# Sign weights held behind the mask addition of the same step: one change to VectorE's order in a fused attention and feed-forward kernel

## The chip, the cores and the metric

The kernel runs on one core of a Trainium2 chip. A core has five engines with an instruction queue each: TensorE (PE, matrix products, with PEld for its weight loads), VectorE (DVE), ScalarE (ACT), GpSimd (POOL) and SyncE (SP, which here only issues DMA transfers). Work between engines is ordered by semaphores. The metric is the device time of one launch in microseconds; lower is better.

## The reference

An image batch of 8 x 32 x 32 x 384 goes through two layers. `x` is float32 throughout.

```python
# layer 0: windowless attention with relative positions, 6 heads of 64
x = x + _L0_conv_ref(_gn(x), qkv_w, qkv_b, proj_w, proj_b, rel_pos_h, rel_pos_w)
# layer 1: causal single-head attention of width 384, then the feed-forward
t = _to_tokens(x)                        # 8 x 1024 x 384
t = t + _L1_attn_ref(_ln_t(t), Wq, Wk, Wv)
t = t + _L1_ffn_ref(_ln_t(t), W1, b1, W2, b2)

def _binarize_weights_groupwise(W):      # 5 groups along the output features
    for g in range(NUM_GROUPS):
        wg = W[g * gs:(g + 1) * gs]
        z = wg - wg.mean()
        Wb = Wb.at[g * gs:(g + 1) * gs].set(sign(z))   # rows beyond 5 * gs stay zero

def _bitlinear(x, W, b):
    y = einsum('btc,oc->bto', x, _binarize_weights_groupwise(W)) + b
    return _quantize_activations_groupwise(y)          # 8 bits, 5 groups along the batch
# feed-forward: _bitlinear to 1536 features, exact GELU, _bitlinear back to 384
```

With 8 images and 5 groups along the batch, each of images 0 to 4 is a group of its own, and images 5 to 7 belong to none: their quantised result stays zero. So the feed-forward matters for images 0 to 4 alone.

## The kernel before

**Order of the images.** One loop goes over the images in the order 5, 0, 1, 2, 3, 4, 6, 7 (`ORDER`); images 0 to 4 (`B_FFN = 5`) also run the feed-forward. Image 5 comes first since it has no feed-forward, so that there is time to make the sign weights.

**Layer 0** (`layer0`, `attend0_fast`). Queries and keys are projected (L438), relative positions are written to DRAM and gathered back as tiles `r` (L484 to L524), values are projected (L536). Attention goes over three pairs of heads and two halves of the tokens. One such half-stage has 8 tiles of scores (L588 for the product, L592 for the positions), their exponentials on ScalarE (L598), additions of the 8 exponentials on VectorE (L603, L605), and the product with the values (L613). The sums over the tiles and their reciprocals of the half-stage before are done between the additions (L622 to L640): L631 multiplies into a PSUM bank `den`, L635, L427 and L428 read it. A residual image is loaded (L106) and `pb` added to it on POOL (L567). Then comes the projection (L386).

**Layer 1** (`attention1`, `attend1_fast`). Layer norm, queries (L734), values (L386 too, as `f_v`), and then eight steps `c` of 128 keys. A step computes its scores (L775), adds the causal mask to the diagonal tile on VectorE (L780), takes exponentials (L782), and lets `values(c - 2)` multiply probabilities with values (L788) and update the residual on VectorE (L789 to L791). Between them stands one step of the next image's group norm (`other`; L338 to L349).

**The sign weights** (`binarize`) are a generator that runs once, in small steps. It loads the raw weights in three pieces of 1.5 MB on POOL's queue (L232), sums them by group on VectorE (L250, 20 sums), forms the means (L256, L258 on POOL, L262), loads the same pieces again, and writes signs over them with two VectorE instructions a block (L272, L273, 30 pairs; L279 clears a rest). Each finished piece is stored to the DRAM tensors `w1s` and `w2s` by SP (L280). It is created in layer 0 of image 5, at pair 2 (`signs.append(binarize(pools))`), and then each step of layer 1 of images 5 and 0 takes two of its steps:

```python
for work in 2 * signs:
    next(work, None)
```

The feed-forward of each image loads the sign weights from DRAM (`sign_weights`, POOL, L862 to L865) and multiplies with them at L895 and L936.

**What sets the order.** The program is written in one order, and a scheduler then places the instructions on each engine's queue by what it reckons to be ready; an instruction can come to stand far earlier than the place where it is written, if its operands allow it. `with tc.issue_after(ins):` adds an edge: each instruction traced inside on the engine of `ins` is placed behind `ins` in that engine's queue, with no semaphore. On a queue, instructions go in order.

**Buffers.** Tiles of 12 KB a partition (`pools.flat`, `pools.image`) come from one pool of 11: `x`, `q`, `k`, `v`, the four `r`, `oT`, `far`, the layer-1 tiles, the raw and sign pieces, the feed-forward's weights and hidden tiles. A tile waits for the last use of the tile that had its buffer before. All PSUM tiles come from one pool of 8 banks (`o_tile`).

Of the kernel before, what the change touches and what calls it, by code (L numbers as in the profile page):

```python
# [15 lines left out]
ALU = mybir.AluOpType  # L16
# [3 lines left out]
P = 128  # L20
# [55 lines left out]
def conv_attn_hybrid(  # L76
# [19 lines left out]
    nc = tc.nc  # L96
# [48 lines left out]
    maskT = const.tile([P, P], F32, name="maskT")  # L145
# [159 lines left out]
    def stages(pools):  # L305
# [120 lines left out]
        def check(total, reciprocal, i):  # L426
            nc.vector.tensor_reduce(seen[:, 0, i : i + 1], total, AX.X, ALU.add)  # L427
            nc.vector.tensor_reduce(seen[:, 1, i : i + 1], reciprocal, AX.X, ALU.add)  # L428
# [333 lines left out]
        def attend1_fast(xt, b, q, xT, v, other, start):  # L762

            room = [pools.flat(f"pr1_{b}_{i}") for i in range(2)]
            tot = pools.small.tile([P, NJ], F32, tag="tot1", name=f"tot1_{b}")
            rt = pools.small.tile([P, NJ], F32, tag="rt1", name=f"rt1_{b}")

            def scores(c):
                at = sum(NJ - i for i in range(0 if c < 3 else 3, c)) * P
                pr = room[c >= 3][:, at : at + (NJ - c) * P]  # L770
                for half in range(c // 4, 2):
                    sc = pools.o_tile(f"s1_{b}_{c}_{half}")
                    lo = max(0, c * P - half * 512)
                    for k in range(NC):
                        nc.tensor.matmul(  # L775
                            sc[:, lo:], xT[:, c // 4, k, ts(c % 4, P)], q[:, half, k, lo:],
                            start=(k == 0), stop=(k == NC - 1),
                        )
                    if half == c // 4:
                        nc.vector.tensor_tensor(sc[:, ts(c % 4, P)], sc[:, ts(c % 4, P)], maskT, ALU.add)  # L780
                    at = half * 512 + lo - c * P
                    nc.scalar.activation(pr[:, at : at + 512 - lo], sc[:, lo:], AF.Exp)  # L782
                return pr

            def values(j):
                av = pools.o_tile(f"av1_{b}_{j}")
                for c in range(j + 1):
                    nc.tensor.matmul(av[:, : C + 1], prs[c][:, ts(j - c, P)], v[:, c, :], start=(c == 0), stop=(c == j))  # L788
                nc.vector.tensor_copy(tot[:, j : j + 1], av[:, C : C + 1])  # L789
                nc.vector.reciprocal(rt[:, j : j + 1], tot[:, j : j + 1])  # L790
                nc.vector.scalar_tensor_tensor(  # L791
                    xt[:, j, :], av[:, :C], rt[:, j : j + 1], xt[:, j, :], ALU.mult, ALU.add
                )

            prs = []
            for c in range(NJ):
                prs.append(scores(c))
                next(other, None)
                for work in 2 * signs:
                    next(work, None)  # L800
                if c >= 2:
                    values(c - 2)
            if b < B_FFN:
                for work in signs:
                    assert next(work, None) is None
                signs.clear()
            start()
            values(NJ - 2)
            values(NJ - 1)
            check(tot, rt, b * PER_IMAGE + PER_IMAGE - 1)  # L810
# [143 lines left out]
        signs = []  # L954
# [92 lines left out]
```

## Time and profile before

| what | before |
|---|---|
| median of 3 runs | 2371.3 us (2369.2 to 2372.32) |
| the profiled execution | 2370.05 us |
| its span | 2367.9 us |
| mean granted PE clock | 0.996 |
| layer 0 of image 5, pairs 1 and 2, from 110 to 193 us | PE's windows are in the prediction |
| sums of raw weights (L250) | 20, from 114.7 to 255.2 us |
| signs (L272, L273) | 30 pairs, from 264.2 to 507.8 us |
| layer 1 steps of image 5 | from 242 to 289 us |
| layer 1 steps of image 0 | from 488 to 536 us |
| first use of the sign weights (L895) | 542.18 us |

The profile's page has, in this order: busy time of each engine with its share of the span, the span in 40 slices (digits are tenths), the DMA queues, the chain of waits that ended last, the costliest groups of instructions, and the DMA issues with the median time from issue to landing. A group reads: line, engine, operation, output<-input, sizes, count, busy us, mean ns of one, idle us of the engine just before it and what ended most of it. Lines are those of the kernel file before; in the changed file, lines from L780 on stand 2 or 3 further down. PE's matmul ends are modelled, and adjacent records overlap.

### The profile page before, as it was taken

What the parts mean: (1) busy time and instruction counts of PE and PEld (TensorE: products, weight loads), DVE (VectorE), ACT (ScalarE), POOL (GpSimd) and SP (SyncE); (2) the same over time, 40 slices, a digit from 0 to 9 for tenths busy, and PEclk for the clock granted to TensorE, in tenths of its full rate; (3) what the DMA queues carried; (4) which work ended last, traced back from release to release, by engine and by line L of the source; (5) the groups of instructions that cost most, each with busy time, mean ns of one, the idle gap of its engine ahead of it and who ended that gap; (6) DMA issues with size and microseconds to landing.
All of it is one profiled execution on the core that took longest, in us unless ns stands there. A gap on an engine that the chain in (4) does not pass through costs nothing.

```text
span 2367.9 us, 26177 instructions
## 1 busy us (share of the span) xinstructions
PE 2332.1 (98%) x9442; PEld 1291.8 (55%) x9442; DVE 1431.8 (60%) x2302; ACT 1042.0 (44%) x1763; POOL 312.2 (13%) x421
## 2 busy tenths in 40 slices
PE   7989999999999999999999999999999999999998
PEld 3445544557644577445684455764457744554454
DVE  3486548754678346685455873567844668525851
ACT  3442146226564146561374622656424656115520
POOL 0320004000230001220002300023000122001300
PEclk9989999999999999999999999999999999999999
DMA  7421363220441011621107311054101172017100
GB/s 163 146 63 54 134 118 96 81 80 1 114 113 68 14 41 44 162 63 40 41 1 145 96 67 41 1 116 114 65 14 41 44 162 63 1 47 137 57 1 29
DMA packets 154795, 169.99 MB, mean 72 GB/s; under 512 B 113408, under 2 KB 126048, under 8 KB 153120
## 3 DMA queue, kind: packets, MB, share of 16 engines
q1 hardware_dynamic: 134416, 98.93, 17.5%
q0 software_dynamic: 17184, 69.22, 9.7%
q8 instruction: 77, 1.26, 0.2%
q10 hardware_dynamic: 3056, 0.08, 0.1%
q14 instruction: 62, 0.51, 0.1%
HBM read 75.38 MB, written 42.47 MB: 50 GB/s over the span
## 4 chain that ended last, share of the span: by engine, by line
PE 95%; DVE 2%; DMA 1%; POOL 0%; issue 0%; ACT 0%; SPq 0%; DVEq 0%; POOLq 0%; ACTq 0%
PE f_s L588 13%; PE f_av L613 13%; PE f_qk L438 11%; PE f_s L775 8%; PE f_av L788 8%; PE f_y L936 7%; PE f_y L895 7%; PE f_pj L386 5%; PE f_v L386 5%; PE f_v L536 5%; PE f_q L734 5%; PE f_s L592 3%; PE f_rel L484 2%; PE f_pt L314 1%; DVE f_sum L605 1%; PE f_den L631 0%
## 5 line engine op out<-in xcount | busy, mean ns | idle before, releaser
L598 ACT ACTIVATE f_pr<-f_s 128x512 f32<-128x512 f32 x768 | 413.8, 595 | 72.3 <-PE f_s L592 64.1
L588 PE MATMUL f_s<-f_q,f_k 64*128 64x512 f32 x1536 | 404.7, 600 | 11.9 <-DVE seen L427 11.9
L605 DVE TENSOR_TENSOR f_sum<-f_sum,f_pr 128x1024 f32<-128x1024 f32 x288 | 364.4, 1265 | 22.4 <-DVE rt L635 0.6
L613 PE MATMUL f_av<-f_pr,f_v 128*64 128x512 f32 x1536 | 339.4, 594 | 0.0
L592 PE MATMUL f_s<-f_r,unit 64*128 64x512 f32 x768 | 311.5, 797 | 0.0
L438 PE MATMUL f_qk<-f_gnT,wqkv_sb 128*128 128x512 f32 x576 | 258.8, 602 | 1.5 <-DVE f_gnT L349 1.5
L588 PEld LDWEIGHTS f_s<-f_q,f_k 64*128 64x128 f32 x1536 | 148.1, 188 | 140.7 <-issue 74.1
L613 PEld LDWEIGHTS f_av<-f_pr,f_v 128*64 128x64 f32 x1536 | 106.3, 137 | 196.4 <-issue 192.4
L775 PE MATMUL f_s<-f_q,f_lnT 128*128 128x512 f32 (+3 forms) x576 | 195.9, 488 | 0.0
L788 PE MATMUL f_av<-f_v,f_pr 128*128 128x385 f32 x576 | 195.3, 486 | 0.0
L438 PEld LDWEIGHTS f_qk<-f_gnT,wqkv_sb 128*128 128x128 f32 x576 | 108.4, 192 | 144.2 <-issue 131.7
L524 POOL DMA_DIRECT2D f_r<-f_far x192 | 102.5, 536 | 462.3 <-DVE f_far L519 418.9
L782 ACT ACTIVATE f_pr<-f_s 128x512 f32<-128x512 f32 (+3 forms) x96 | 47.1, 491 | 263.8 <-DVE f_s L780 217.6
L788 PEld LDWEIGHTS f_av<-f_v,f_pr 128*128 128x128 f32 x576 | 108.2, 190 | 77.3 <-issue 11.5
L775 PEld LDWEIGHTS f_s<-f_q,f_lnT 128*128 128x128 f32 x576 | 102.0, 190 | 77.8 <-issue 54.1
L899 ACT ACTIVATE f_h<-f_y,b_sb 128x256 f32<-128x256 f32 x240 | 100.9, 471 | 67.3 <-PE f_y L895 67.3
L906 DVE TENSOR_REDUCE am<-f_h 128x1 f32<-128x1024 f32 (+2 forms) x80 | 71.6, 947 | 96.1 <-ACT f_h L899 96.1
L734 PE MATMUL f_q<-f_lnT,wqk 128*128 128x512 f32 x288 | 127.5, 592 | 0.0
L386 PE MATMUL f_pj<-wproj_sb,f_oT 128*128 128x384 f32 x384 | 127.3, 488 | 0.0
L592 PEld LDWEIGHTS f_s<-f_r,unit 64*128 64x128 f32 x768 | 76.9, 188 | 91.2 <-issue 90.7
L386 PE MATMUL f_v<-wv_sb,f_lnT 128*128 128x384 f32 x384 | 126.5, 486 | 0.0
L536 PE MATMUL f_v<-wqkv_sb,f_gnT 128*128 128x384 f32 x384 | 125.1, 486 | 0.0
(153 smaller groups left out, 3018.6 us busy)
## 6 DMA issues: line engine op xcount, KB each, us to landing
f_far<-f_far SPq DMA_DIRECT2D x48, 512.0 KB, 3.3
f_r<-f_far POOLq DMA_DIRECT2D x192, 128.0 KB, 3.9
f_r<-f_far SPq DMA_DIRECT2D x192, 128.0 KB, 3.2
f_gnT<-in_xT SPq DMA_DIRECT2D x24, 512.0 KB, 4.6
f_x<-in_x SPq DMA_DIRECT2D x32, 384.0 KB, 8.1
out_y<-f_x POOLq DMA_DIRECT2D x28, 384.0 KB, 4.5
f_far<-f_far SPq DMA_DIRECT2D x128, 64.0 KB, 5.1
f_w1a<-w1s POOLq DMA_DIRECT2D x5, 1536.0 KB, 6.9
```

What stands on the lines that cost most here:

```text
L386: nc.tensor.matmul(ps[:, :C], xT[:, k, ts(j, P)], w[:, k, cols], start=(k == 0), stop=(k == NC - 1))
L438: nc.tensor.matmul(made[half], wqkv_sb[:, i, ts(m, P)], xT[:, i, ts(half, 512)], start=(i == 0), stop=(i == NC - 1))
L536: nc.tensor.matmul(ps, keys[:, i, j // 2, j % 2], wqkv_sb[:, i, 2 * C :], start=(i == 0), stop=(i == NC - 1))
L588: nc.tensor.matmul(sc[par], k[rows[par], p, ts(c, P)], q[rows[par], p, ts(half, 512)], start=True, stop=False)
L592: last_matmul[0] = nc.tensor.matmul(sc[par], unit[rows[par], c // 2 % 2].rearrange("i h w -> i (h w)"), r[2 * (c // 4) + c % 2][rows[par], ...
L598: last_exp[0] = nc.scalar.activation(pr[:, ts(par, 512)], sc[par], AF.Exp).ins
L605: adds.append(nc.vector.tensor_tensor(total, total, pr, ALU.add).ins)
L613: last_matmul[0] = nc.tensor.matmul(av[ts(par, HD), :], v[:, c, ts(2 * p + par, HD)], pr[:, ts(par, 512)], start=(c == 0), stop=(c == NJ - 1),
L734: nc.tensor.matmul(ps, wqk[:, k, ts(m, P)], xT[:, half, k, :], start=(k == 0), stop=(k == NC - 1))
L775: nc.tensor.matmul(sc[:, lo:], xT[:, c // 4, k, ts(c % 4, P)], q[:, half, k, lo:], start=(k == 0), stop=(k == NC - 1),)
L788: nc.tensor.matmul(av[:, : C + 1], prs[c][:, ts(j - c, P)], v[:, c, :], start=(c == 0), stop=(c == j))
L895: nc.tensor.matmul(ps, w1k[i // 2][:, ts(m, P)], xs[i % 2][:, half, i // 2, :], start=(i == 0), stop=(i == 2 * NC - 1))
```

## The change

The 2 steps of the sign weights that a step of layer 1 takes are traced inside `issue_after` of that step's mask addition. So each of their VectorE instructions is placed behind that addition on VectorE's queue. Their POOL and SP instructions (loads, all-reduce, stores) get no such edge. At the end of image 0's steps, the check that the generator is used up also lets it run out.

```diff
@@ scores(c)
                     if half == c // 4:
-                        nc.vector.tensor_tensor(sc[:, ts(c % 4, P)], sc[:, ts(c % 4, P)], maskT, ALU.add)
+                        masked[0] = nc.vector.tensor_tensor(
+                            sc[:, ts(c % 4, P)], sc[:, ts(c % 4, P)], maskT, ALU.add
+                        ).ins
@@ attend1_fast
-            prs = []
+            prs, masked = [], [None]
             for c in range(NJ):
                 prs.append(scores(c))
                 next(other, None)
-                for work in 2 * signs:
-                    next(work, None)
+                with tc.issue_after(masked[0]):
+                    for work in 2 * signs:
+                        next(work, None)
                 if c >= 2:
                     values(c - 2)
             if b < B_FFN:
                 for work in signs:
-                    assert next(work, None) is None
+                    assert all(done for done in work)
                 signs.clear()
```

## The prediction

> **What bounds the kernel now.** I read the page's busy shares and chain first, then the waits of the stretch in which PE has holes, then PE's and VectorE's timelines there, last a table of windows.
>
> ```profile
> PE 2332.1 (98%) x9442; PEld 1291.8 (55%) x9442; DVE 1431.8 (60%) x2302; ACT 1042.0 (44%) x1763; POOL 312.2 (13%) x421
> ...
> PE   7989999999999999999999999999999999999998
> ...
> PE 95%; DVE 2%; DMA 1%; POOL 0%; issue 0%; ACT 0%; SPq 0%; DVEq 0%; POOLq 0%; ACTq 0%
> ```
>
> PE is busy 98% of the span and carries 95% of the chain, so only what stops or slows PE counts. Apart from the start and the end, one slice of forty is below nine tenths: the third, 118 to 178 us. The waits from 95 to 160 us (waiting line, releaser: total us, times, longest):
>
> ```profile
> DVE sums_w L250 <- DMA f_w<-in_w1T: 18.9, 2, 13.9
> ...
> PE f_s L588 <- DVE seen L427: 11.9, 2, 7.4
> ```
>
> PE waits twice for VectorE, and VectorE waits twice for a load of raw feed-forward weights. PE's timeline (start, us, line, idle before it), then VectorE's:
>
> ```profile
> 113.40 1.02 PE L588 MATMUL f_s<-f_q,f_k 64*128 64x512 f32 x2
> 121.77 1.22 PE L588 MATMUL f_s<-f_q,f_k 64*128 64x512 f32 x1 [7.36 <-DVE seen L427]
> ...
> 144.72 2.08 PE L588 MATMUL f_s<-f_q,f_k 64*128 64x512 f32 x4 [4.54 <-DVE seen L427]
> ```
>
> ```profile
> 98.94 1.84 DVE L605 TENSOR_TENSOR f_sum<-f_sum,f_pr 128x1024 f32<-128x1024 f32 x1
> 114.71 0.79 DVE L250 TENSOR_REDUCE sums_w<-f_w 128x1 f32<-128x614 f32 x1 [13.92 <-DMA f_w<-in_w1T]
> ...
> 121.55 0.17 DVE L427 TENSOR_REDUCE seen<-f_den 128x1 f32<-128x16 f32 x1
> ...
> 132.62 4.09 DVE L250 TENSOR_REDUCE sums_w<-f_w 128x1 f32<-128x307 f32 x10 [5.00 <-DMA f_w<-in_w1T]
> ...
> 144.40 0.17 DVE L427 TENSOR_REDUCE seen<-f_den 128x1 f32<-128x16 f32 x1
> ```
>
> VectorE stands from 100.8 to 114.7 at a weight sum (L250) whose load POOL issued only at 107.34. Behind it are the additions of L605 and the reduction L427, which frees the PSUM bank that PE's next score tile needs. PE starts again 0.2 to 0.3 us after each L427. The windows compare these two half-stages of image 5 (scores of one pair and half, then values) with the same two of image 0:
>
> ```profile
> 110.02:136.65 26.63, 19.27 (x86) 10.07 (x85) 16.80 (x28) 12.29 (x19) 2.62 (x3) 0.87 0.36 130
> 136.65:160.06 23.41, 18.88 (x86) 8.17 (x84) 22.46 (x24) 9.23 (x17) 7.15 (x10) 0.85 0.26 69
> 373.80:389.87 16.07, 16.07 (x87) 6.91 (x85) 13.43 (x15) 12.31 (x19) 6.51 (x8) 1.00 0.12 29
> 389.87:405.93 16.06, 16.06 (x87) 6.93 (x85) 15.53 (x18) 9.22 (x17) 6.99 (x9) 1.00 0.38 103
> ```
>
> The same PE work takes 26.63 + 23.41 = 50.04 us in image 5 and 16.07 + 16.06 = 32.13 us in image 0. The granted clock (third number from the end) is 0.87 and 0.85 against 1.00.
>
> **What the Trainium skill says.** "PSUM — Partial Sum Buffer", Engine vs sequencer instructions: VectorE's queue is strict FIFO. The trace agrees: L605 had its operands and still stood 13.92 us behind L250. "TensorE: Matmul & The Clock Gate", What's actually happening: an idle window of about 3.4 us halves PE's clock until PE has been busy as long. The trace agrees in kind: both holes are longer, and afterwards the rel-pos matmuls (L592), two at a time, take 1.45 us where they take 0.80 in image 0. "Trainium Kernel Development and Optimization", Key Constraints: transfers of SP, ACT and POOL share 16 DMA engines. So the moved transfers could delay others; their share between 300 and 560 us leaves room.
>
> **The change part by part.** The order in which the changed kernel is built shows that no L250 is left in layer 0: all 20 sums stand in layer 1 of image 5, each behind a mask addition (L780). The hold binds VectorE only; POOL's loads are free, and move where buffers come free.
>
> *Removed: the two stops.* 50.04 − 32.13 = **17.91 us**: 11.90 of idle (7.36 + 4.54) and 6.0 of slow matmuls after it. Next in line on VectorE are additions that ran without stopping PE in image 0. The second load of raw weights now stands on POOL behind pair 2's rel-pos pieces. Those are due before PE's scores at 142 (160.06 − 17.91); by image 0's spacing they land at about 137, and the weights have until 253.
>
> *Added to image 5's layer 1* (times of before; all shift together): 15 sums, 3.8 us for five of 614 columns and 2.0 each for the fives of 307 and 304: 7.8 us. Six pairs of sign instructions (L272, L273; 0.85 us a pair: 12.7 us for 15 pairs) leave for image 0: −5.1. VectorE was busy 29.72 of the 47 us from 242 to 289, now 32.4. Step by step:
> - Four sums (2.9 us) follow mask 0 at 245.3 and end at 248.2; L345 starts 0.5 late, but its square root waits for a table load until 249.44. Mask 1's scores come at 249.69: nothing lost.
> - One sum, the three normalisations and four sums of 307: mask 2 at 254.6 for 253.65. Its probabilities are first needed at 263.7: hidden.
> - Masks 3 to 6 wait for PE as before, within 0.3 us. The last sum ends at 265.0, the mean (POOL, 0.48 us) at 266; it is first used at 272.
> - Twenty sign instructions now stand as one block between mask 6 (271.7) and mask 7: 0.3 + 10 pairs at 0.74 start to start = 7.7 us. Mask 7 comes at 279.7 for 275.63, its exponential ends at 280.5. PE needs it for the last term of the last value tile, at about 288.5: 8 us of cover. The block also delays the residual update of value tile 4; its bank is next needed at 299.
>
> *Added to image 0's layer 1:* the six pairs, 5.1 us, fill VectorE's waits around masks 0 and 1 (1.79 + 2.32 + 1.89 us idle): mask 2 at 499.9 for 499.85. Nothing.
>
> *Buffers and queues.* The second piece of sign weights keeps its buffer through image 0's layer 0.
> - Image 0's residual load (SP, L106) must now wait for pair 1's pieces on POOL: 358.03 + 3.68 + 3.9 landing = 365.6 for 361.31. POOL's additions (L567) end at 382.3, one multiply at 384.5; POOL's next piece comes at 389.78: 5 us of cover.
> - The first load of sign weights for image 0 (POOL, L862) takes that buffer. It was issued at 455.93; now it waits for the piece (done 499.9) and its stores (at most 5.0 to land): issued 505, landed 512 (6.9). Behind it the next load waits for the last store: sign block done about 511, stored 516, landed 521 (4.5). PE needs them at 542.18 and 543.19: 30 and 22 us of cover. SP is empty from 428 to 508, so the moved stores push nothing.
>
> *Unknown:* whether the changed order stops PE for an instant that these sums do not show. Below: 1 us more gained, the spread of the half-stages being 0.1. Above: 4.1 us, the slip of mask 7, were its cover gone. I take 0, since each sum above ends before PE needs it.
>
> *Sum.* The profiled execution took 2370.05 us (span 2367.9 and 2.15 around it), 1.25 below the median of 2371.3. 2370.05 − 17.91 = 2352.1 for such an execution, so **2353.4 us** beside the median.
>
> **The rivals.**
> 1. *Only the idle time comes back.* PE runs slow in these half-stages for another reason, say the 86 to 195 GB/s of transfers: −11.9, **2359.4 us**. Against it: image 0 runs at clock 1.00 beside 103 GB/s, and in image 5 from 160 on the clock is 1.00 again.
> 2. *The stop moves.* VectorE stops in layer 1, at L279 or L262, for the sign load or the mean, with mask 7 and three residual updates behind it. It decides once VectorE resumes after 280 instead of 272; each us more costs PE one. 26 us late gives no change, **2371 us**. Against it: the mean is 6 us early, the sign load, free once the projection has read its buffer (209.5), is there by about 217.
> 3. *Slower: sign weights late for image 0.* The load that now shares a buffer with the second piece lands after 542, and PE waits for it; by the two stops of before, each us of idle brings half a us of slow matmuls (6.0 for 11.9), so it decides from 12 us late on, landing at 555. If the signs ended only with layer 1 (537.65, the last L360) and stores (4.4 + 3.3 + 5.0) and loads (6.9 + 4.5) went one after another, the second load would land at 562: 19 idle and 9 slow, less 17.9: 10 slower, **2381 us**. Against it: 30 and 22 us of cover, with stores and signs an engine apart.
>
> That the change doesn't do what it says is excluded by the built order. What stays open is only whether VectorE's waits end as reckoned.
>
> **How the numbers follow.** Forecast (17.9, with the bounds −1 and +4.1): 0.86. Rival 1: 0.08. Rival 2 within 0.2%: 0.03. Rival 3: 0.03. 0.2% is 4.7 us, about what a measurement of this kernel can tell from no change. The forecast and rival 1 are faster: 0.94; same 0.03; slower 0.03. The range begins at the forecast less 1 and the 2 us by which the runs lie under their median: 2350.5. It ends at 2359.6, which takes in the bound of 4.1 and rival 1.
>
> **What would show it.** In the profile after: no wait of PE's L588 for L427; the two half-stages at 16.1 us each, clock 1.00; all L250 after the first L780 with no idle before them for a transfer; mask 7 about 4 us later against PE; L862 of image 0 about 50 us later against PE, and no idle before f_y. Wrong if PE shows new idle in the layers 1 of images 5 or 0, or at the first f_y.

## The result, and the profile after

The changed kernel takes **2351.88 us** (median of 4 runs, 2350.82 to 2352.87) where the kernel before takes 2371.55 beside it: a ratio of 0.9919, 95% interval 0.9901 to 0.9936. That is 19.7 us less. In the profiled executions it is 2350.82 for 2370.05. In this file L784 is the exponential of layer 1, L790 the value product, L793 the residual update, L865 the first load of sign weights, L898 the first product of the feed-forward.

Of the page, the lines that answer to those of before (busy shares, PE's forty slices, the chain by engine):

```profile
PE 2324.9 (99%) x9442; PEld 1288.2 (55%) x9442; DVE 1433.9 (61%) x2302; ACT 1041.7 (44%) x1763; POOL 316.6 (13%) x421
...
PE   7999999999999999999999999999999999999998
...
PE 99%; DVE 1%; DMA 0%; issue 0%; ACT 0%; DVEq 0%
```

The 8 in the third slice is a 9, and PE's share of the chain is 99% for 95%. All of PE's waits in the whole span (waiting line, releaser: total us, times, longest):

```profile
PE f_gmean L336 <- DVE gmv L333: 10.9, 1, 10.9
PE f_bad L201 <- DVE worst L199: 1.9, 1, 1.9
PE f_qk L438 <- DVE f_gnT L349: 1.5, 1, 1.5
PE f_gvar L344 <- DVE gd L341: 0.7, 1, 0.7
PE f_den L631 <- DVE few L624: 0.3, 1, 0.3
```

The row of L588 for L427 (11.9 us) is gone, and none has come in its place: but for 0.3 us at L631, in another image, what is left lies at the start and the end. One more wait is gone with it, of 0.35 us: before, PE also waited at L631 at 192.59 us, ahead of the projection of image 5. The windows of the two half-stages of image 5 (the stretch and its length, busy us of PE, PEld, DVE, ACT, POOL with counts, granted clock, DMA share, GB/s):

```profile
108.75:124.81 16.06, 16.06 (x87) 6.81 (x85) 15.60 (x19) 12.27 (x19) 4.85 (x5) 1.00 0.40 126
124.81:140.86 16.05, 16.05 (x87) 6.80 (x85) 15.54 (x17) 9.17 (x17) 8.16 (x12) 1.00 0.63 187
```

50.04 us have become 32.11: **17.93 us**, where 17.91 were forecast, at clock 1.00, with 187 GB/s beside it in the second. Another 1.27 us lie ahead of these windows, at the start of the kernel (108.75 for 110.02), in work that the change does not touch. From 193 us to the end PE's products stay 19.0 to 20.1 us earlier than before, and the spans differ by 19.1, so nothing later in the kernel gained or lost more than a us. The rest is taken up at the end.

In layer 1 the sign weights' block stands where it was reckoned. Masks 6 and 7 before:

```profile
271.66 0.29 DVE L780 TENSOR_TENSOR f_s<-f_s,maskT 128x128 f32<-128x128 f32 x1
...
275.63 0.30 DVE L780 TENSOR_TENSOR f_s<-f_s,maskT 128x128 f32<-128x128 f32 x1
```

And after, VectorE, then ScalarE, then PE, from their timelines:

```profile
252.10 0.30 DVE L780 TENSOR_TENSOR f_s<-f_s,maskT 128x128 f32<-128x128 f32 x1 [0.28 <-PE f_s L775]
252.31 0.24 DVE L262 TENSOR_SCALAR mean_w<-mean_w 128x5 f32<-128x5 f32 x2
...
260.05 0.28 DVE L780 TENSOR_TENSOR f_s<-f_s,maskT 128x128 f32<-128x128 f32 x1
```

```profile
260.37 0.28 ACT L784 ACTIVATE f_pr<-f_s 128x128 f32<-128x128 f32 x1 [7.55 <-DVE f_s L780]
```

```profile
257.75 11.83 PE L790 MATMUL f_av<-f_v,f_pr 128*128 128x385 f32 x36
269.42 10.46 PE L438 MATMUL f_qk<-f_gnT,wqkv_sb 128*128 128x512 f32 x24
```

Mask 7 comes 7.95 us after mask 6 instead of 3.97, so 4.0 later; its exponential ends at 260.65; PE goes through its value products without a hole, and the last of them, which needs it, starts at about 269.1.

### The profile page after: what moved, and what is told of

It reads as the page before. It is cut to its first block, busy times and chain, and to the rows that moved or that the text cites. A ratio compares the mean times of both kernels' runs of the same rounds, so it can differ in the third digit from the quotient of the medians.

```text
span 2348.8 us, 26174 instructions
## 1 busy us (share of the span) xinstructions
PE 2324.9 (99%) x9442; PEld 1288.2 (55%) x9442; DVE 1433.9 (61%) x2302; ACT 1041.7 (44%) x1763; POOL 316.6 (13%) x421
## 4 chain that ended last, share of the span: by engine, by line
PE 99%; DVE 1%; DMA 0%; issue 0%; ACT 0%; DVEq 0%
PE f_s L588 14%; PE f_av L613 14%; PE f_qk L438 11%; PE f_s L775 8%; PE f_av L790 8%; PE f_y L939 7%; PE f_y L898 7%; PE f_pj L386 5%; PE f_v L386 5%; PE f_v L536 5%; PE f_q L734 5%; PE f_s L592 4%; PE f_rel L484 2%; PE f_pt L314 1%; PE f_den L631 0%; DMA f_gnT<-in_xT 0%
## 5 line engine op out<-in xcount | busy, mean ns | idle before, releaser
L588 PE MATMUL f_s<-f_q,f_k 64*128 64x512 f32 x1536 | 399.0, 595 | 0.0
L438 PE MATMUL f_qk<-f_gnT,wqkv_sb 128*128 128x512 f32 x576 | 257.4, 600 | 1.5 <-DVE f_gnT L349 1.5
L588 PEld LDWEIGHTS f_s<-f_q,f_k 64*128 64x128 f32 x1536 | 145.7, 186 | 127.4 <-issue 67.3
L790 PE MATMUL f_av<-f_v,f_pr 128*128 128x385 f32 x576 | 195.3, 486 | 0.0
L438 PEld LDWEIGHTS f_qk<-f_gnT,wqkv_sb 128*128 128x128 f32 x576 | 108.0, 191 | 143.2 <-issue 131.5
L784 ACT ACTIVATE f_pr<-f_s 128x512 f32<-128x512 f32 (+3 forms) x96 | 47.1, 491 | 267.7 <-DVE f_s L780 220.7
L790 PEld LDWEIGHTS f_av<-f_v,f_pr 128*128 128x128 f32 x576 | 108.2, 190 | 77.3 <-issue 11.5
```

Source lines behind the costliest of these rows:

```text
L438: nc.tensor.matmul(made[half], wqkv_sb[:, i, ts(m, P)], xT[:, i, ts(half, 512)], start=(i == 0), stop=(i == NC - 1))
L588: nc.tensor.matmul(sc[par], k[rows[par], p, ts(c, P)], q[rows[par], p, ts(half, 512)], start=True, stop=False)
```

## The experiments

Theory: the whole gain is that VectorE no longer waits, in layer 0 of image 5, for loads of raw weights with L427 queued behind the wait. Rivals: the signs' place carries part of it; the work of the sums, not their wait, held L427 up; the two stops of PE are one; and, for the size, whether slow matmuls go with the number of stops or with their length.

| kernel | median us | ratio to before (95%) | PE's new or remaining stops over 1 us |
|---|---|---|---|
| the change | 2351.88 | 0.9919 (0.9901 to 0.9936) | none |
| sums_held | 2352.0 | 0.9920 (0.9907 to 0.9934) | none |
| signs_held | 2371.07 | 0.9999 (0.9991 to 1.0008) | 6.87 and 5.77 |
| pieces23_held | 2362.65 | 0.9965 (0.9951 to 0.9978) | 7.28 |
| piece1_held | 2352.88 | 0.9931 (0.9918 to 0.9945) | 2.59 |
| resident_sums | 2353.18 | 0.9926 (0.9912 to 0.9939) | 1.65 |
| block_plus1 | 2351.84 | 0.9920 (0.9907 to 0.9934) | none |
| block_plus4 | 2351.38 | 0.9917 (0.9903 to 0.9930) | none |
| pinned_plus4 | 2361.16 | 0.9959 (0.9945 to 0.9972) | 6.26 |
| load_late5 | 2373.98 | 1.0013 (1.0006 to 1.0019) | 17.1 in four |
| load_again4 | 2361.45 | 0.9965 (0.9951 to 0.9978) | 6.26 |
| load_again7 | 2384.08 | 1.0056 (1.0042 to 1.0069) | 29.17 |
| after_busy_start | 2354.0 | 0.9930 (0.9915 to 0.9944) | at the start |

The medians of the kernel before, taken beside these kernels, lie between 2370.78 and 2371.55.

### Which half of the change carries it: sums_held and signs_held

`hold[0]` is the mask addition of the step; in one kernel the sums alone are traced behind it, in the other the signs alone.

```diff
+                with tc.issue_after(hold[0]):                          # sums_held
+                    nc.vector.tensor_reduce(part[...], w[...], AX.XY, ALU.add)
...
+                    with tc.issue_after(hold[0]):                      # signs_held
+                        nc.vector.tensor_scalar(above, wg, m, None, ALU.is_gt)
+                        nc.vector.scalar_tensor_tensor(wg, wg, m, above, ...)
```

> The kernel before with only the 20 sums (L250) behind the masks; the signs keep their free place. Theory (the whole gain is VectorE's wait for raw weights leaving layer 0 of image 5): no wait of L588 for L427, half-stages of 16.1 us, 2352 us as the changed kernel. Rival (the place of the signs carries part of it, since without a hold they come as 10 pairs before mask 7 and 10 pairs behind it): 2355 to 2360.

> The kernel before with only the signs (L272, L273) behind the masks; the sums stay in layer 0. Theory: both stops of PE stay (7.4 and 4.5 us, half-stages 26.6 and 23.4), 2371 us as before, within 1. Rival (the signs' place carries part of the gain): 2365 or less.

Measured: 2352.0 and 2371.07. The sums alone give the whole gain and the signs alone give none. So half of the change, the hold on the signs, does nothing for the time here: with or without it they fill VectorE's idle time.

### Whether the stops are separate: pieces23_held and piece1_held

The hold of sums_held under a condition; `held(on)` is `tc.issue_after(hold[0])` where `on` is true and nothing otherwise.

```diff
+                with held(not (n_out == FF and times[0] == 0)):        # pieces23_held
+                    nc.vector.tensor_reduce(part[...], w[...], AX.XY, ALU.add)
...
+                with held(n_out == FF and times[0] == 0):              # piece1_held
+                    nc.vector.tensor_reduce(part[...], w[...], AX.XY, ALU.add)
```

> The kernel before with the sums of the second and third loads behind the masks; the first load's 5 sums stay in layer 0. Theory (the two stops are separate): the stop of 7.4 us stays with its slow stretch (half-stage 26.6), the second half-stage falls from 23.4 to 16.1 but for what is left of the slow stretch: 2371.5 - 7.3 = 2364, 2363 to 2367. Rival (the second stop is only an echo of the first, VectorE never having caught up): PE stops a second time, 2369 to 2371.

> The kernel before with only the 5 sums of the first load behind the masks. The second load's 10 sums now stand in the half-stage after the one they stood in, behind its fourth addition, at about 135 us, and their load, issued at about 135, lands at about 142.5: VectorE stands some 7 us. Theory (a stop of PE is VectorE's standing time less some 6.5 us of cover, as in 13.9 less 7.4): PE stops 0 to 2 us, the first half-stage is 16.1 us, 2352 to 2355 us. Rival (each load waited for in layer 0 costs PE a stop of its own, 4.5 us and a slow stretch): 2359 to 2361.

The windows of the same two half-stages where the first load's sums stay in layer 0:

```profile
110.17:136.75 26.58, 19.30 (x87) 10.10 (x85) 21.51 (x27) 12.32 (x19) 2.63 (x3) 0.87 0.35 127
136.75:152.80 16.05, 16.05 (x86) 6.80 (x84) 15.52 (x19) 9.17 (x17) 7.18 (x10) 1.00 0.38 102
```

One half-stage has its stop as before (26.58 us, clock 0.87), the next is whole: 2362.65 us. The second stop was not an echo of the first. 7.28 of the 10.52 us that the first half-stage has too much are idle, 3.24 are matmuls that run slow.

Where the second load's sums stay instead, VectorE does stand, but PE does not at that place. VectorE's timeline, then PE's:

```profile
139.48 0.47 DVE L256 TENSOR_REDUCE sums_w<-f_w 128x1 f32<-128x307 f32 x1 [5.23 <-DMA f_w<-in_w1T]
```

```profile
175.46 0.29 PE L637 MATMUL f_den<-few,fold 128*64 128x16 f32 x4 [2.59 <-DVE few L630]
```

(L256 is L250, L637 is L631 in that file.) A wait of 5.23 us behind the fourth addition of a half-stage is covered there. What VectorE lost comes out at the end of layer 0, where nothing stands between its last additions and PE: 2.59 us. The time is 2352.88, in the range of the theory, though the theory had put the stop, if any, a half-stage earlier. No slow stretch follows: against the changed kernel's profile, PE's products lose 2.6 us at this stop, its idle time and no more. By the median only 1.0 us is left at the end of the kernel. In the profile, the fastest of five runs that spread over 5.2 us, most of the 2.6 us is made up bit by bit up to 1902 us and at no one place, so the runs do not tell this from the spread of executions.

### Wait or work: resident_sums

```diff
-                    part[...], w[:, :, ts(g, n_out // NG)], AX.XY, ALU.add
+                    part[...], there[:, :, ts(g, n_out // NG)], AX.XY, ALU.add
```

`there` is a view of the projection weights for the first two loads; the edges that hold the places are left out here. The loads themselves still run.

> The kernel before, but the 15 sums of the first two loads read the projection weights, which have long been on the chip, in tiles of the same shapes (so the means are of other numbers); they keep their places in VectorE's queue in layer 0, by an edge behind the same additions. It keeps their work there, 8 us, and takes only their wait away. Theory (the wait, not the work): no stop of PE, half-stages of 16.1 us, 2351 to 2354 us. Rival (the 8 us of work between the additions holds L427 up as well): PE stops, 2357 us or more.

Measured: 2353.18 us, no wait of the score products for VectorE. The sums' work, still between the additions of layer 0, cost PE one wait of 1.65 us at L631, and the median 1.3. The other 18 us were the wait.

### How far mask 7 may slip: block_plus1, block_plus4, pinned_plus4

```diff
                     for work in 2 * signs:
                         next(work, None)
+                    if b == ORDER[0] and c == 6:
+                        for i in range(4):          # 1 in block_plus1
+                            nc.vector.tensor_reduce(idle[:, i : i + 1], wqkv_sb.rearrange("p k c -> p (k c)"), AX.X, ALU.add)
```

> The changed kernel with one more VectorE instruction between masks 6 and 7 of image 5 (a sum over 3456 columns of a resident tile into a scratch tile, some 4.3 us by the rate of L250). Theory (mask 7 has 8.4 us of cover left: its exponential ends at 260.65, PE's last value product starts at 269.1): mask 7 comes 4.3 us later, PE does not stop, 2352 us within 1. Rival (the cover is less than reckoned, since PE or the residual updates wait earlier): 2354 to 2357.

> The changed kernel with four such instructions between masks 6 and 7 of image 5, some 17 us. Theory: mask 7 comes at 277, PE stops for 17 less 8.4 = 8.7 us at the last value product and then runs slow for some 3 us, as after the stop of 7.3 us in the run that kept only the first load's sums in layer 0: 2363 to 2364 us. Rival (the slow stretch grows with the idle time, half a us for each): 2365. Rival (mask 7 is not what PE waits for): 2352.

One more instruction moves mask 7 from 260.05 to 264.35 (0.7 us of this is the later start of that execution, 3.6 the instruction) and costs nothing, as reckoned. Four move it to 275.58, and the time is still 2351.38: the theory missed by 12 us. PE's timeline says why:

```profile
256.85 13.13 PE L790 MATMUL f_av<-f_v,f_pr 128*128 128x385 f32 x40
269.81 7.03 PE L438 MATMUL f_qk<-f_gnT,wqkv_sb 128*128 128x512 f32 x16
276.68 0.81 PE L790 MATMUL f_av<-f_v,f_pr 128*128 128x385 f32 x2
277.32 3.60 PE L438 MATMUL f_qk<-f_gnT,wqkv_sb 128*128 128x512 f32 x8
```

The program was not the same on PE. The scheduler put 16 projections of the next image ahead of the last value product. Presumably it reckoned with a late mask; the trace shows the order alone. The experiment had changed two things. So it was run again with these projections held behind the last value product, which gives PE's order of the changed kernel:

```diff
+                    with tc.issue_after(last_value[0]) if pools.fast and b == AFTER[ORDER[0]] else contextlib.nullcontext():
                         nc.tensor.matmul(made[half], wqkv_sb[:, i, ts(m, P)], ...)
```

> The changed kernel with the four more VectorE instructions between masks 6 and 7 (block_plus4), and PE's order held as in the changed kernel: the next image's projections (L438) stay behind the last value product, as they do there. Mask 7 then comes 15.5 us later than in the changed kernel, as it did in block_plus4. Theory (8.4 us of cover by that order): PE stops for 15.5 - 8.4 = 7.1 us at the last value product, then a slow stretch of some 3.2 us: 2362 us. Rival (mask 7 is not what PE waits for): 2352. Rival (the residual updates held with it stop PE later too): over 2364.

```profile
275.69 1.65 PE L793 MATMUL f_av<-f_v,f_pr 128*128 128x385 f32 x2 [6.26 <-ACT f_pr L787]
277.14 12.63 PE L441 MATMUL f_qk<-f_gnT,wqkv_sb 128*128 128x512 f32 x24
```

(L793 is the value product in that file, L441 the projection.) Mask 7 comes 22.45 us after mask 6 here, 14.5 more than in the changed kernel (the four took 14.9 us together, a little less than reckoned), and PE stops for 6.26 us: 8.2 us were covered. The 24 projections behind the stop take 12.63 us instead of 10.46: 2361.16 us, 9.3 over the changed kernel. So the 8 us of cover in the prediction hold, for a fixed order on PE. A scheduler that knows of the delay had another 7 us of work to put there.

### The price of late sign weights: load_late5, load_again4, load_again7

```diff
+            for _ in range(5 if b == 0 else 0):                        # load_late5
+                nc.gpsimd.tensor_tensor(a1, flat, flat, ALU.add)
...
+            for _ in range(7 if b == 0 else 0):                        # load_again7; 4 in load_again4
+                nc.gpsimd.dma_start(out=a1, in_=w1s[:, : 2 * half])
             nc.gpsimd.dma_start(out=a1, in_=w1s[:, : 2 * half])
```

`flat` is a view of the projection weights.

> The changed kernel, with POOL's load of w1a for image 0 put behind five additions on POOL that write its tile (3072 columns each, some 9.4 us by the rate of L567): issued at about 537.5 instead of 484.7, landed at about 544.5, where PE needs it at 522.6. It prices the prediction's slower rival. Theory now: 22 us of idle and a slow stretch of fixed length, some 3 us: 2377 us. Rival (the price that the prediction used, half a us of slow matmuls for each us of idle): 2352 + 22 + 11 = 2385 us. Rival (the weights are not what PE needs first): 2352.

Measured: 2373.98 us, near the theory's 2377, and for another reason: the load was issued at 525.23 and PE came to it at 544.45 without a wait. VectorE's timeline beside POOL's additions (the second fence):

```profile
502.12 11.80 DVE L376 TENSOR_SCALAR f_xn<-f_x,lmv,lrs 128x384 f32<-128x384 f32 x2
513.85 0.15 DVE L791 COPY tot<-f_av 128x1 f32<-128x1 f32 x1
513.92 5.86 DVE L376 TENSOR_SCALAR f_xn<-f_x,lmv,lrs 128x384 f32<-128x384 f32 x1
```

```profile
502.54 5.32 POOL L867 TENSOR_TENSOR f_w1a<-wqkv_sb 128x3072 fp32r<-128x3072 f32 x1
```

Each L376 takes 5.4 to 6.0 us where it takes 0.46 in the changed kernel: as long as one POOL addition. The Trainium skill, "SBUF — State Buffer", SBUF: two separate sides, says that GpSimd and certain VectorE instructions (in a two-port mode, or with two SBUF inputs) share one pair of ports as an exclusive lock, held for a whole instruction. The lengths agree with it; that L376 is of that kind no run here shows. PE waited 17.1 us for these L376 and what is queued behind them, so the run says nothing of late weights. The wait is in four stops (2.28, 5.39, 4.88 and 4.57 us) with 0.6 to 0.9 us of products between them. The delay was made again with transfers alone, each load of the tile waiting for the one before.

> The changed kernel with the load of w1a for image 0 done five times over into its tile, each behind the landing of the one before (some 7.4 us each; no POOL computation beside VectorE). The last lands at about 528, where PE needs it at 522.6. Theory (a slow stretch of about 3 us per stop): 5.6 us of idle and 3 of slow matmuls, 2360.5 us. Rival (half a us of slow matmuls for each us of idle): 2360.3, the same here. Rival (enough cover left): 2352.

> The same with eight loads, the last landing at about 550: 27.8 us of idle. Theory (the slow stretch after a stop is some 3 us, whatever the stop's length): 2351.9 + 27.8 + 3 = 2382.7 us. Rival (the price that the prediction used, half a us of slow matmuls for each us of idle): 2351.9 + 27.8 + 13.9 = 2393.6 us.

Measured: 2361.45 and 2384.08 us. PE's timelines (L900 is L898), first with five loads, then with eight:

```profile
530.17 0.77 PE L900 MATMUL f_y<-f_lnT,f_w1a 128*128 128x512 f32 x1 [6.26 <-DMA f_w1a<-w1s]
```

```profile
551.62 0.77 PE L900 MATMUL f_y<-f_lnT,f_w1a 128*128 128x512 f32 x1 [29.17 <-DMA f_w1a<-w1s]
552.19 0.63 PE L900 MATMUL f_y<-f_lnlo,f_w1a 128*128 128x512 f32 x1
...
556.03 0.52 PE L900 MATMUL f_y<-f_lnT,f_wrest 128*128 128x512 f32 x1
556.38 0.39 PE L900 MATMUL f_y<-f_lnlo,f_wrest 128*128 128x512 f32 x1
```

Products start 0.43 us apart until about 556.1 and 0.23 apart from there. The slow stretch is 4.5 us after 29.17 us of idle, and 4.5 us (530.17 to 534.7) after 6.26. The cost of each stop, by medians over the changed kernel, and beside it how much later than in the changed kernel's profile PE's products are behind the stop, less how much later they were ahead of it:

| stop | idle us | cost by medians | beyond the idle | later by the traces | beyond the idle |
|---|---|---|---|---|---|
| load_again4 | 6.26 | 9.6 | 3.3 | 8.6 | 2.3 |
| pinned_plus4 | 6.26 | 9.3 | 3.0 | 9.4 | 3.1 |
| pieces23_held | 7.28 | 10.8 | 3.5 | 10.5 | 3.2 |
| load_again7 | 29.17 | 32.2 | 3.0 | 31.5 | 2.4 |

The medians carry the spread of whole executions (1.4 to 4.9 us within these kernels), so the traces decide. For load_again7: its transposes ahead of the stop start at 520.98 where the changed kernel's start at 521.40, and its 14th product behind it at 556.84 where the changed kernel has it at 525.72; 31.12 and 0.42 make 31.54. A stop that stands alone costs its length and **2.3 to 3.2 us**, and at one and the same place as much for 29.17 us of idle as for 6.26. For the two load_again runs 2.1 of the 2.3 to 2.4 are the slow rate itself (11 products at 0.43 instead of 0.23). Why the two others cost 0.8 us more was not taken apart. The four stops of load_late5, close together, cost 4.2 us in all beyond their idle time, by its trace, and not four times the price.

### Whether it is PE's standing alone: after_busy_start

```diff
+            keep_busy(36)       # 36 products of a resident 128x128 tile into a bank that nobody reads
             ps = pools.o_tile(f"gmean_{b}")
             nc.tensor.matmul(ps[:, 0:1], over_group, mv[:, 0:1], start=True, stop=True)
+            keep_busy(4)
...
+            keep_busy(10)       # behind the product of the variance
```

> The changed kernel with 50 products of a small resident tile (128x128, into a bank that nobody reads) in PE's wait at the start: 36 before the product of the group mean (L336), 4 behind it, 10 behind that of the variance (L344). It asks whether the slow stretch after a stop and the slow first projections are one thing. In six runs so far the first 24 products of L438 took 12.0 to 13.6 us, the same 24 for image 0 took 10.46. Theory (PE's clock is low because PE stood, and products nobody needs raise it as well as others): the first 24 take about 10.5 us, the whole 2350 us, 1.5 to 3 below the changed kernel's in a profile. Rival (the first products are slow for what they load or for the chip's start): 2352 us, or a little more by the products in the way.

PE's timeline at the start, in the changed kernel and then in this one (L339 is an added product, L447 is L438):

```profile
14.27 12.20 PE L438 MATMUL f_qk<-f_gnT,wqkv_sb 128*128 128x512 f32 x24 [1.53 <-DVE f_gnT L349]
```

```profile
4.25 9.73 PE L339 MATMUL f_warm<-over_group 128*128 128x128 f32 x72 [4.25 <-POOL over_group L164]
...
15.08 2.48 PE L339 MATMUL f_warm<-over_group 128*128 128x128 f32 x20
17.39 10.47 PE L447 MATMUL f_qk<-f_gnT,wqkv_sb 128*128 128x512 f32 x24
```

The first 24 projections take 10.47 us, like those of image 0: products that nobody needs keep PE at its rate as well as others. But the added ones took longer than their place (two records each; the 36 end at about 13.9, where the group mean was there at 10.9), so the projections start at 17.39 instead of 14.27, and the kernel takes 2354.0, 2.1 more than the changed kernel. With fewer of them some 1.5 to 3 us should be had, an estimate from the 12.01 to 13.60 us of the other profiles less these 10.47; no run shows that.

## Why the prediction was right

It forecast 2353.4 us, range 2350.5 to 2359.6, and 0.94 for faster; 2351.88 were measured.

- *The stops removed, 17.91 us*: 17.93 in the windows. That the sums alone carry it (sums_held), their wait and not their work (resident_sums), and each stop by itself (pieces23_held) is shown.
- *Rival 1, slow from transfers*: fallen. 187 GB/s ran beside a half-stage at clock 1.00, and in the run that left one stop only the half-stage with the stop is slow. Slow matmuls came after each stop of 4.5 us or more, and else only at the start.
- *Rival 2, the stop moves into layer 1*: fallen. VectorE uses the mean (L262) at 252.31, right behind mask 6, without a wait.
- *Layer 1 of image 5*: VectorE was to be busy 32.4 of 47 us and was 32.91; mask 2 was to slip by 1 us and slipped 0.83 (234.92 against PE, by the 19.56 us that mask 0 moved); masks 3 to 6 kept their places; mask 7 was to slip 4.1 and slipped 3.98. Its cover of 8 us is borne out by pinned_plus4 (8.2), for the order that PE has.
- *Queues and buffers*: POOL's load L865 was to be issued at 505 on the clock of before; it was at 484.70, which is 504.3 there (19.55 later, by which the first L898 moved). The load behind it came at 497.86, 517.4 there, for 516. PE's first L898 at 522.63 did not wait.
- *The second raw-weights load behind pair 2's pieces*: as reckoned, PE's scores of pair 2 at 140.86 did not wait.
- *POOL's residual additions*: their load was issued at 346.48, which is 366.0 on the clock of before, for 365.6. They ended at 358.8, 378.3 there, for 382.3: the later issue cost the additions 0.3 us, not the 4.3 that were reckoned. POOL's next piece came at 390.1 there, for 389.78.
- *The term that was wrong: rival 3's price.* It took half a us of slow matmuls for each us of idle from the sum of two stops (6.0 for 11.9). It does not grow with the idle time: 2.3 us beyond 6.26 us of idle and 2.4 beyond 29.17 at the place that rival 3 speaks of (load_again7 took 2384.08; half a us for each us of idle would have been 2393.6). The Trainium skill, "TensorE: Matmul & The Clock Gate", What's actually happening, which the prediction drew on, says as much: the slow time ends when PE has been busy for one window, some 3.4 us by the page; it was 4.5 here. So rival 3 would have decided from some 15.5 us late on (17.9 less 2.4), not from 12, and its case of 19 us of idle would have been some 3.5 us slower than before, not 10. The forecast did not rest on it.

What the sum does not hold: the medians differ by 19.7, 1.8 more than the windows. Of this 0.35 is PE's wait at L631 at 192.59 us, which the prediction did not list. It is there in the kernel before, in signs_held and in resident_sums, and as 2.59 us in piece1_held, where the second load's sums stand in layer 0, and in no run that holds these sums. In the two profiles another 1.27 is the start of the kernel. Over 13 profiles of these kernels, one of each, the first 24 products of L438 took between 12.01 and 13.60 us; with the changed code it was 12.01 to 13.47, and the kernel before had the slowest. So the 1.27 looks like the chance of two executions, which the forecast could not hold. In signs_held, which has both stops too, the two half-stages took 50.48 us against 50.04, so the stops themselves are not the same to half a us. Together these can make the difference; that they make it in the medians was not shown.

## What to carry to other kernels

A scheduler that may move an instruction forward places it by what it expects of its operands; an instruction that waits for a transfer, moved ahead on an in-order queue, makes all that is queued behind it wait too, however unimportant it is itself. Look for the engine that waits for a DMA while the bound engine waits for it, and hold only those instructions behind a later point of that queue. Price a stop of PE that stands alone as its length and a fixed amount (2.3 to 3.2 us here, for 6 to 29 us of idle), and when an experiment delays something, see that the order on the other engines stayed the same.

## What the runs showed of the hardware beyond that

- *One price, whatever the length.* After stops of 6.26 and 29.17 us PE ran at 0.43 us for each product of 512 columns instead of 0.23, for 4.5 us in both. After 2.59 us (piece1_held) it did not: the 42 products of the projection behind it took 13.81 us, as in the changed kernel. The shortest stop standing alone with slow products behind it was one of 4.54 us, in the kernel before; what lies between the two was not measured.
- *The same at the start.* The first 24 projections took 12.01 to 13.60 us, and 10.47 with PE kept busy by products without a use, so a spread of 1.6 us between executions lies there.
- *Large POOL additions and VectorE.* Four L376 of 0.46 us took 5.4 to 6.0 each while POOL worked on 3072 columns in 5.3 us. Over 384 columns (L567) an addition took 1.00 us at the median in the kernel before, and up to 1.98, so 8 us or more for the same 3072 columns in eight.
